# Layer 1's attention: weighted values summed eight heads at a time, more weight buffers, and the end of a half as a stage of its own

## The chip, the cores and the metric

The kernel runs on one core of one Trainium2 chip. Its time is the device time of one launch in microseconds (us). Of several runs the median is given; one more execution was taken with the hardware profiler, and all rows of the profile come from that one.

## What is computed

Two layers run over 16 sequences (b) of 512 tokens and 128 channels, all in float32. Each layer is a layer norm, then the sum of a sequence mixer, a feed-forward part and the input itself.

```python
# layer 0: a memory MLP trained by a scan over chunks (the mixer), and:
q, k, v = split(conv(x) @ wqkv.T + bqkv)                   # 16 heads of 8 channels
ctx  = softmax(q @ k.T / sqrt(8)) @ v                      # no mask
x    = layernorm(x + ctx @ wo.T + bo)
x    = layernorm(x + sum_e probs[e] * (relu(x @ w1[e]) @ w2[e]))   # 8 experts, all of them

# layer 1
ctx  = causal_attention(q, k, v);  q2 = conv(ctx)
out  = causal_attention(q2, k, v) @ out_w.T + out_b        # a second look at the same k and v
ffn  = top-8 of 32 experts, gathered and scattered by token
```

So layer 0 has one attention per sequence and layer 1 has two, both masked so that a token sees itself and what is before it.

## The kernel before

The program is written as Python generators, called stages here. Class `Turns` runs them: in one turn every stage that is alive is advanced by one step. Each stage has a priority. Those of priority 0 step first, then those of priority 1, then the others from 2 to 6. TensorE gets its instructions in exactly this order (`ORDERED`); for the other engines a scheduler orders them, with the edges that `issue_after` adds: what stages of priority 1 and up give VectorE comes behind the last maximum of priority 0 (`newest`), and what stages of priority 2 and up give GpSimd comes behind the last mask of priority 1 (`cleared`). The program before has 1281 turns, counted as it is built.

Attention is done in halves of 8 heads (c is 0 or 1), and each half is looked at twice:

- The first look is `tops` with `largest`, priority 0. A step computes scores with the queries as weights (L190, `s<-kx,qx`) and takes the maximum of each row on VectorE (L387 with the mask in one instruction, or L395 and L396). Its maxima are carried into two extra rows of the queries.
- The second look is `back` with `weighted`, priority 1. A step computes the scores again, transposed (`s<-qx,kx`), and ScalarE takes the exponential into a weight tile `e` (L461). In layer 1 GpSimd then zeroes what the mask hides (L465).

Each look has one score tile of two banks in PSUM, so a step of a look cannot begin before the engine that reads the scores has finished with the step before it. `widths` says what a step covers. In layer 0 a half takes 16 steps of two heads and 512 queries. In layer 1 the mask shortens it: four steps of two heads by 512 queries, four of two heads by 384, two of four heads by 256, and one of eight heads by 128, 11 steps in all. The looks of layer 1 follow each other without a gap: a sequence takes 4 halves, or 44 turns (`TBB`).

The weighted values are TensorE matmuls of 32 columns each (`pc<-e,vp`), four heads side by side in the four column groups of the array. A float32 matmul appears in the profile as two passes, so four heads are eight rows. They are summed in one bank, `pc`, of which there is one (lock `ctx`). Function `tail(n)` issues them: behind the scores of a step, if four heads or more are waiting in the list `old`, their four values go out; I call this a visit. Weight tiles come from a ring of three. At the end of a half the same stage, still at priority 1, issues what is left (four heads a turn), copies `pc` to `cs` (L437, ScalarE), transposes it (`tpc`, L241) and divides by the sums on VectorE (L485, L486). Meanwhile the next half's `weighted` has begun, and steps later in the same turn.

The large filler of TensorE's time is layer 0's experts, stage `ffn` of priority 6, which runs through nearly all of the program. A unit of it is `phe<-x1T,ew` (L190, 512 columns, with a relu on ScalarE, L565) or the four matmuls of `pye<-ew,hTe` (L573). How many units a turn gets is a matter of credit in estimated nanoseconds:

```python
credit[0] = min(credit[0] + TURN - load_ns[0], 4000)       # TURN = 2750
n = int(max(credit[0] + 500, 0) // 1000)
```

So a turn in which other stages gave TensorE much work gets fewer units, and the turns behind it get more. Where `ffn` is not at work, `fill` adds matmuls that nobody reads.

Stage `middle` (layer 0's end and layer 1's routing) uses pool `mid`, which is open from the end of the scan (turn 481) to turn 1167. Then `moe` takes its place; it gathers and scatters tokens with DMAs that GpSimd issues.

Of the kernel before, what the change touches and what calls it, by code (L numbers as in the profile page):

```python
# [9 lines left out]
F32 = mybir.dt.float32  # L10
# [7 lines left out]
P = 128  # L18
# [55 lines left out]
def bc(ap, axis, n):  # L74

    u = ap.unsqueeze(axis)
    shape = list(u.shape)
    shape[axis] = n
    return u.to_broadcast(shape)
# [3 lines left out]
def network(ctx: ExitStack, tc: tile.TileContext, a, out):  # L83
# [26 lines left out]
    def load(pool, name, shape):  # L110
        t = pool.tile(shape, F32, bufs=1, name="sb_" + name)
        nc.sync.dma_start(t, a[name])
        return t
# [21 lines left out]

    pools, done, locks, clock, newest, cleared, held, read, cell = {}, {}, set(), [0], [None], [None], [0], [0], []

    def mark(*m):
        done[m] = clock[0]

    def after(*marks, lag=0):

        while not all(m in done and clock[0] >= done[m] + lag for m in marks):
            yield

    def acquire(name):
        while name in locks:
            yield
        locks.add(name)
# [7 lines left out]
    def room():  # L157

        while held[0] >= pools["work"]:
            yield  # L160
# [6 lines left out]
    def drop():  # L167

        read[0] += 1
# [12 lines left out]
    def mm(o, lhsT, rhs, start=True, stop=True):  # L182
        n = int(np.prod(rhs.shape[1:]))
        if lhsT.dtype == FR:
            load_ns[0] += 0.5 * (0.45 * n + 105)
        else:
            t = 0.42 * n if lhsT.shape[-1] == 32 and n >= P else 2 * max(0.834 * n, 110)
            load_ns[0] += t
            array_ns[0] += t
        nc.tensor.matmul(o, lhsT=lhsT, rhs=rhs, start=start, stop=stop)  # L190
# [46 lines left out]
    def turn4(src, name="tp"):  # L237

        tp = work(name)
        for t in range(4):  # L240
            nc.tensor.transpose(tp[:, t * P : (t + 1) * P], src(t), ident)  # L241
        load_ns[0] += 900
        array_ns[0] += 900
        return tp
# [12 lines left out]

    def ends(stage, name):
        yield from stage
        mark(name)  # L260

    def idle(n):
        for _ in range(n):
# [87 lines left out]
    def widths(causal):  # L351

        for i in range(TB):
            n = S if not causal else S - i * P
            per = {S: 1, 3 * P: 1, 2 * P: 2, P: 4}[n]
            for t in range(0, NH, per):
                yield i, n, per, t
# [58 lines left out]
            )  # L416
        yield

    def weighted(slot, vp, c, causal, cn):

        q, k, _ = slot
        yield from acquire("p2")
        cnv = cn.rearrange("p t (a c j d) -> p (t a) c j d", c=2, j=2, d=DH)
        old, ends = [], []
        got = []

        def values(heads):
            for kt, n, t, r, e in heads:
                g = 2 * (t % 2) + r
                j = t // 2  # L430
                mm(
                    got[0][32 * g : 32 * g + 32, S - n :], vp[:, kt, 4 * g + 2 * c + j, :], e,
                    start=(kt == 0 and j == 0), stop=(kt == TB - 1 and j == 1),
                )
            if kt == TB - 1 and t == NH - 1:
                cs = att.tile([P, S], F32, tag="cs", bufs=1, name="cs")
                nc.scalar.copy(cs, got[0])  # L437
                locks.remove("ctx")
                ends.append(cs)

        def tail(n):
            if not got and "ctx" not in locks:
                locks.add("ctx")
                got.append(pools["ps"].tile([P, 512], F32, tag="ctx", bufs=1, name="pc"))
            for _ in range(n):
                if got and len(old) >= 4:
                    locks.add("values")
                    values([old.pop(0) for _ in range(4)])

        for kt, n, per, t in widths(causal):  # L450
            while len(old) >= 4 and not got and "ctx" in locks:
                yield
            s = pools["ps"].tile([P, 2, 512], F32, tag="p2", bufs=pools["p2"], name="s2")
            sv = s[:, :, 0 : per * n].rearrange("p r (i n) -> p r i n", i=per)
            for u in range(per):
                for r in range(2):
                    rr = slice(64 * r, 64 * r + 64)
                    mm(sv[:, r, u, :], k[rr, t + u, kt * P : (kt + 1) * P], q[rr, t + u, S - n :])
            tail(2)
            e = att.tile([P, 2, 512], F32, tag="e", bufs=pools["e"], name="e")  # L460
            nc.scalar.activation(e[:, :, 0 : per * n], s[:, :, 0 : per * n], AF.Exp, scale=SCALE)  # L461
            ev = e[:, :, 0 : per * n].rearrange("p r (i n) -> p r i n", i=per)
            if causal:
                for r in range(2):
                    cleared[0] = nc.gpsimd.affine_select(  # L465
                        out=ev[:, r, :, 0:P], in_=ev[:, r, :, 0:P], pattern=[[0, per], [1, P]],
                        compare_op=ALU.is_ge, fill=0.0, base=0, channel_multiplier=-1,
                    )
            for u in range(per):
                for r in range(2):  # L470
                    old.append((kt, n, t + u, r, ev[:, r, u, :]))
            yield
        locks.remove("p2")
        free_slots.append(slot)
        while old:
            tail(1)
            yield
        cs = ends[0]
        yield from room()
        held[0] += 1  # L480
        tp = turn4(lambda t: cs[:, t * P : (t + 1) * P], "tpc")
        yield
        tv = tp.rearrange("p (b j x) -> p b j x", j=2, x=16)
        rec = sm.tile([P, TB * NG, 2], F32, tag="rec", name="rec")
        nc.vector.reciprocal(rec, tv[:, :, :, DH])  # L485
        nc.vector.tensor_tensor(cnv[:, :, c], tv[:, :, :, 0:DH], bc(rec, 3, DH), ALU.mult)  # L486
        drop()
        yield
# [10 lines left out]
    def ffn(b):  # L499
# [106 lines left out]
        yield  # L606
        nc.sync.dma_start(x1d[0, b], flat(ac))
        mark("ffn", b)
        yield

# [5 lines left out]
    att = main.enter_context(tc.tile_pool(name="att", bufs=1))  # L616
    fa = main.enter_context(tc.tile_pool(name="fa", bufs=2))
    ff = main.enter_context(tc.tile_pool(name="ff", bufs=1))
    ps = main.enter_context(tc.tile_pool(name="psum", bufs=1, space=PSUM))
    pools.update(ps=ps, p1=1, p2=1, work=3, e=3, pairs=True)  # L620
    Wt = Pack(load(fa, "pb", [P, sum(PB.values())]), PB)
    cell.append(Wt.t)
    row.update(load_rows(fa, "rows0", ROWS0))
# [416 lines left out]
    def tops(layer, b, i, c):  # L1040
        yield from after(("rows", layer, b, i))
        got, z = [], live[layer, b]
        yield from take(free_slots, got)
        z[i, c] = got[0]
        rows_in(got[0], c, z["r2"] if i else z["rq"], z["rk"])
        yield from idle(3)
        yield from largest(got[0], layer == 1)
        mark("tops", layer, b, i, c)

    def back(layer, b, i, c):  # L1050
        yield from after(("tops", layer, b, i, c), lag=4)
        yield from after(("vals", layer, b))
        z = live[layer, b]
        if c == 0:
            z["cn"] = (l1 if layer else fa).tile([P, TB, D], F32, tag="cn", bufs=2, name="cn")
        yield from weighted(z[i, c], z["vp"], c, layer == 1, z["cn"])
        mark("back", layer, b, i, c)

    def post0(b):
        yield from after(("back", 0, b, 0, 0), ("back", 0, b, 0, 1))  # L1060
# [28 lines left out]
    def experts0():  # L1089
        for b in range(B):  # L1090
            yield from ffn(b)

    TA = 32
    turns = Turns(
        [(60, 6, experts0())]
        + [(b * TA, 4, front0(b)) for b in range(B)]
        + [(b * TA + 4 + 16 * c, 0, tops(0, b, 0, c)) for b in range(B) for c in range(2)]
        + [(b * TA + 30 + 16 * c, 1, back(0, b, 0, c)) for b in range(B) for c in range(2)]
        + [(b * TA + 60, 4, post0(b)) for b in range(B)]
    )  # L1100
    with tc.tile_pool(name="p0", bufs=1) as p0:
        stage = norm0(p0)
        turns.stages.append((0, 3, ends(stage, "norm0")))
        turns.run(until=lambda: ("norm0",) in done)
    with tc.tile_pool(name="scan", bufs=1) as s1:
        turns.stages.append((turns.turn, 3, ends(scan(s1), "scan")))
        turns.run(until=lambda: ("scan",) in done)


# [286 lines left out]
    )  # L1396
    with tc.tile_pool(name="mid", bufs=1) as mid:
        turns.stages += [(t0 + b * TBB, 4, middle(mid, b)) for b in range(B)]
        turns.run(until=lambda: ("xw", B - 1) in done)
    with tc.tile_pool(name="mo", bufs=2) as mo:  # L1400
        turns.stages.append((turns.turn, 3, moe(mo)))
        turns.stages += [(turns.turn, 5, total(b)) for b in range(B)]
        turns.run()
# [111 lines left out]
```

## Time and profile before

| | us |
|---|---|
| median of 3 runs | 4081.94 |
| lowest and highest | 4064.09, 4087.86 |
| the profiled execution, its own time | 4071.58 |
| its span | 4069.8 |

| engine | busy us | share of the span |
|---|---|---|
| TensorE (PE) | 3646.2 | 90% |
| VectorE (DVE) | 2368.5 | 58% |
| ScalarE (ACT) | 2201.1 | 54% |
| GpSimd (POOL) | 1681.3 | 41% |

A row of the profile names the line, the engine, the operation and out<-in. A line such as L190 is that of a helper (`mm`), so the matmuls are told apart by their tiles: `s<-kx,qx` first look, `s<-qx,kx` second look, `pc<-e,vp` weighted values. Matmuls overlap in the array and their ends are modelled, so what one costs is read from the distance between starts.

### The profile page before, as it was taken

To read this page: it belongs to the slowest core of one execution; us is meant where nothing else is said; L and a number is where in the kernel's file an instruction comes from. 1 tells how busy PE (TensorE), PEld (TensorE's weight loads), DVE (VectorE), ACT (ScalarE), POOL (GpSimd) and SP (SyncE) were. 2 spreads that over 40 slices of the span, in tenths; PEclk is the share of its full clock that TensorE was granted. 3 is DMA by queue.
4 is the path that set the end of the run, shared out by engine and by line. 5 is a ranking of instruction groups with operands and counts; after the bars stand their busy time and mean duration, and the time that the engine had idled before them with its cause. 6 is when DMAs were issued, how large, how long until landed. Compare 5 with 4: busy or idle time off the path is not lost.

```text
span 4069.8 us, 62831 instructions
## 1 busy us (share of the span) xinstructions
PE 3646.2 (90%) x22668; PEld 1974.2 (49%) x22668; DVE 2368.5 (58%) x5165; ACT 2201.1 (54%) x3686; POOL 1681.3 (41%) x2598
## 2 busy tenths in 40 slices
PE   5998899888999998999999999999999999987877
PEld 2544454444544444455555555555555555543443
DVE  3575656665565555564566655666656666676651
ACT  1355655566557775555555555555555555542332
POOL 7334534455333544134333442333334423434563
PEclk6799999999999999999999999999999999997888
DMA  4222222122223333333333333333333343323334
GB/s 155 62 62 62 70 57 77 57 68 64 75 75 93 108 96 108 101 105 110 90 111 103 114 81 111 108 100 95 111 101 107 87 117 106 94 69 98 70 69 131
DMA packets 271222, 374.22 MB, mean 92 GB/s; under 512 B 42392, under 2 KB 116800, under 8 KB 270144
## 3 DMA queue, kind: packets, MB, share of 16 engines
q1 hardware_dynamic: 263744, 363.38, 30.7%
q0 software_dynamic: 7168, 6.82, 1.0%
q8 instruction: 180, 2.95, 0.3%
q14 instruction: 130, 1.06, 0.1%
HBM read 236.85 MB, written 133.25 MB: 91 GB/s over the span
## 4 chain that ended last, share of the span: by engine, by line
PE 62%; DVE 15%; POOL 7%; ACT 6%; DMA 5%; issue 5%; SPq 0%; POOLq 0%; ACTq 0%; DVEq 0%
PE s L190 16%; PE pye L573 10%; PE phe L190 9%; PE pc L190 9%; DVE nm L396 7%; DVE s L395 3%; ACT e L461 2%; PE pgr L190 2%; POOL e L465 1%; PE tp L241 1%; DVE s L387 1%; PE fill L197 1%; PE po L190 1%; PE pj L190 1%; DMA fin<-ao 1%
## 5 line engine op out<-in xcount | busy, mean ns | idle before, releaser
L461 ACT ACTIVATE e<-s 128x1024 f32<-128x1024 f32 (+1 forms) x1216 | 1190.6, 979 | 836.5 <-PE s L190 796.0
L396 DVE TENSOR_REDUCE nm<-s 128x2 f32<-128x1024 f32 (+1 forms) x704 | 861.9, 1224 | 664.6 <-PE s L190 657.5
L387 DVE CUSTOM_DVE_ANT_0 s<-s,sb_const 128x512 f32<-128x512 f32 (+1 forms) x1024 | 647.6, 632 | 663.9 <-PE s L190 646.4
L465 POOL TENSOR_SCALAR_AFFINE_SELECT e<-e 128x128 f32<-128x128 f32 (+2 forms) x1408 | 464.4, 363 | 1140.9 <-ACT e L461 1133.0
L190 PE MATMUL s<-kx,qx 64*128 64x512 f32 (+3 forms) x3072 | 627.6, 435 | 180.9 <-DVE nm L396 99.4
L190 PE MATMUL pc<-e,vp 128*32 128x512 f32 (+3 forms) x6144 | 712.4, 511 | 52.4 <-POOL e L465 51.3
L190 PEld LDWEIGHTS s<-kx,qx 64*128 64x128 f32 x3072 | 278.7, 189 | 754.0 <-issue 288.9
L573 PEld LDWEIGHTS pye<-ew,hTe 128*128 128x128 f32 x4096 | 517.2, 193 | 212.1 <-issue 195.6
L573 PE MATMUL pye<-ew,hTe 128*128 128x128 f32 x4096 | 572.7, 283 | 0.5 <-DVE cn L486 0.5
L190 PE MATMUL phe<-x1T,ew 128*128 128x512 f32 x1024 | 553.5, 624 | 6.9 <-DVE vp L345 1.9
L190 PE MATMUL s<-qx,kx 64*128 64x512 f32 (+3 forms) x3072 | 536.1, 373 | 21.1 <-ACT e L461 15.3
L565 ACT ACTIVATE hTe<-phe,sb_cols 128x512 f32<-128x512 f32 x512 | 353.1, 690 | 272.5 <-PE phe L190 272.1
L190 PEld LDWEIGHTS s<-qx,kx 64*128 64x128 f32 x3072 | 290.7, 190 | 124.2 <-issue 64.6
L581 POOL TENSOR_TENSOR ac<-ac,y 128x512 f32<-128x512 f32 x128 | 165.4, 1292 | 387.0 <-ACT y L580 386.8
L395 DVE TENSOR_TENSOR s<-s,sb_const 128x256 f32<-128x256 f32 (+1 forms) x384 | 199.4, 519 | 178.8 <-PE s L190 166.5
L190 PEld LDWEIGHTS pc<-e,vp 128*32 128x32 f32 x6144 | 137.6, 109 | 264.7 <-issue 152.2
L190 PEld LDWEIGHTS phe<-x1T,ew 128*128 128x128 f32 x1024 | 158.2, 193 | 113.3 <-issue 84.6
L580 ACT ACTIVATE y<-pye,pr 128x128 f32<-128x128 f32 x512 | 146.8, 368 | 51.0 <-PE pye L573 50.0
L387 DVE DVE_READ_ACCUMULATOR2_ANT nm<- 128x1 f32 x1024 | 145.0, 142 | 0.0
L197 PE MATMUL fill<-sb_pb,sb_const 128*128 128x512 f32 (+3 forms) x256 | 135.9, 621 | 8.8 <-DMA sb_pb<-in_pb 7.8
L437 ACT COPY cs<-pc 128x512 f32<-128x512 f32 x96 | 56.2, 585 | 61.1 <-PE pc L190 59.4
L410 ACT CAST m<-tpm 16x512 fp32r<-16x512 f32 x96 | 54.6, 569 | 59.4 <-PE tpm L408 59.4
(285 smaller groups left out, 4049.0 us busy)
## 6 DMA issues: line engine op xcount, KB each, us to landing
ew<-in_ew SPq DMA_DIRECT2D x256, 256.0 KB
kx<-rk SPq DMA_DIRECT2D x192, 256.0 KB
qx<-rq SPq DMA_DIRECT2D x128, 256.0 KB
rq<-hi SPq DMA_DIRECT2D x64, 256.0 KB
rq<-lo SPq DMA_DIRECT2D x64, 256.0 KB
rk<-hi SPq DMA_DIRECT2D x64, 256.0 KB
rk<-lo SPq DMA_DIRECT2D x64, 256.0 KB
qx<-r SPq DMA_DIRECT2D x64, 256.0 KB
```

The costliest lines, as they stand in the source:

```text
L190: nc.tensor.matmul(o, lhsT=lhsT, rhs=rhs, start=start, stop=stop)
L197: nc.tensor.matmul(o[:, 0:n], lhsT=ident, rhs=cell[0][:, 0:n], start=True, stop=True)
L387: newest[0] = nc.vector.tensor_tensor_reduce(out=sv[:, r, 0, :], in0=sv[:, r, 0, :], in1=row["caus"][:, S - n :], scale=1.0, scalar=-BIG, ...
L395: nc.vector.tensor_tensor(dg, dg, bc(row["caus"][:, S - P :], 1, per), ALU.add)
L396: newest[0] = nc.vector.tensor_reduce(nm[:, qt, :, t : t + per], sv, AX.X, ALU.max)
L437: nc.scalar.copy(cs, got[0])
L461: nc.scalar.activation(e[:, :, 0 : per * n], s[:, :, 0 : per * n], AF.Exp, scale=SCALE)
L465: cleared[0] = nc.gpsimd.affine_select(out=ev[:, r, :, 0:P], in_=ev[:, r, :, 0:P], pattern=[[0, per], [1, P]], compare_op=ALU.is_ge, fill= ...
L565: nc.scalar.activation(hs[i], ph, AF.Relu, bias=col("fb", i))
L573: nc.tensor.matmul(pye[0][:, t, :], lhsT=h[:, t * P : (t + 1) * P], rhs=w2[e][:, f, :], start=(f == 0 and t == 0), stop=(f == 3), skip_gro ...
L580: nc.scalar.mul(y[:, t, :], pye[0][:, t, :], pr[:, t, e : e + 1])
L581: nc.gpsimd.tensor_tensor(ac, ac, y, ALU.add)
```

## The change

Three things are changed. While pool `mid` is open, values go out eight heads at a time (two groups of four behind each other) and not four (`heads`). In the same stretch the weight tiles come alternately from the ring of three in `att` and from a second ring of three in `mid`; the set `lent` holds the heads whose weights lie in `mid`, and the pool is not closed before they are used. And in both layers, for the whole program, the end of a half becomes a stage `summed` of priority 2, which starts in the turn after `weighted` is done: in a turn it steps behind both looks. Its values go out up to eight heads a turn as well.

```diff
-        def tail(n):
+        def tail(least):
             if not got and "ctx" not in locks:
                 locks.add("ctx")
                 got.append(pools["ps"].tile([P, 512], F32, tag="ctx", bufs=1, name="pc"))
-            for _ in range(n):
-                if got and len(old) >= 4:
-                    locks.add("values")
+            if got and len(old) >= least:
+                locks.add("values")
+                for _ in range(min(len(old) // 4, 2)):
                     values([old.pop(0) for _ in range(4)])
 
-        for kt, n, per, t in widths(causal):
-            while len(old) >= 4 and not got and "ctx" in locks:
+        for i, (kt, n, per, t) in enumerate(widths(causal)):
+            while len(old) >= pools["heads"] and not got and "ctx" in locks:
                 yield
...
-            tail(2)
-            e = att.tile([P, 2, 512], F32, tag="e", bufs=pools["e"], name="e")
+            tail(pools["heads"])
+
+            pool = pools["weights"][i % len(pools["weights"])]
+            e = pool.tile([P, 2, 512], F32, tag="e", bufs=3, name="e")
...
         locks.remove("p2")
         free_slots.append(slot)
+        turns.stages.append((turns.turn, 2, ends(summed(old, tail, last, c, cnv), name)))
+
+    def summed(old, tail, last, c, cnv):
+
         while old:
-            tail(1)
-            yield
-        cs = ends[0]
+            tail(4)
+            yield
+        cs, = last
         yield from room()
...
-    pools.update(ps=ps, p1=1, p2=1, work=3, e=3, pairs=True)
+    pools.update(ps=ps, p1=1, p2=1, work=3, weights=[att], heads=4, pairs=True)
...
     with tc.tile_pool(name="mid", bufs=1) as mid:
         turns.stages += [(t0 + b * TBB, 4, middle(mid, b)) for b in range(B)]
+        pools.update(weights=[att, mid], heads=8)
         turns.run(until=lambda: ("xw", B - 1) in done)
+        pools.update(weights=[att], heads=4)
+        turns.run(until=lambda: not lent)
```

More of the change, by code (lines that the diff above doesn't have):

```diff
@@ L136, in network @@
     pools, done, locks, clock, newest, cleared, held, read, cell = {}, {}, set(), [0], [None], [None], [0], [0], []
+    lent = set()
     def mark(*m):
@@ L259, in ends @@
         yield from stage
-        mark(name)
+        mark(*name)
     def idle(n):
@@ L417, in largest, with weighted @@
         yield
-    def weighted(slot, vp, c, causal, cn):
+    def weighted(slot, vp, c, causal, cn, name):
         q, k, _ = slot
@@ L423, in weighted @@
         cnv = cn.rearrange("p t (a c j d) -> p (t a) c j d", c=2, j=2, d=DH)
-        old, ends = [], []
+        old, last = [], []
         got = []
         def values(heads):
-            for kt, n, t, r, e in heads:
+            for head in heads:
+                kt, n, t, r, e = head
+                lent.discard(id(head))
                 g = 2 * (t % 2) + r
@@ L438, in values @@
                 locks.remove("ctx")
-                ends.append(cs)
-        def tail(n):
+                last.append(cs)
+        def tail(least):
             if not got and "ctx" not in locks:
@@ L471, in weighted @@
                     old.append((kt, n, t + u, r, ev[:, r, u, :]))
+                    if pool is not att:
+                        lent.add(id(old[-1]))
             yield
@@ L1055, in back @@
             z["cn"] = (l1 if layer else fa).tile([P, TB, D], F32, tag="cn", bufs=2, name="cn")
-        yield from weighted(z[i, c], z["vp"], c, layer == 1, z["cn"])
-        mark("back", layer, b, i, c)
+        yield from weighted(z[i, c], z["vp"], c, layer == 1, z["cn"], ("back", layer, b, i, c))
     def post0(b):
@@ L1102, in network @@
         stage = norm0(p0)
-        turns.stages.append((0, 3, ends(stage, "norm0")))
+        turns.stages.append((0, 3, ends(stage, ("norm0",))))
         turns.run(until=lambda: ("norm0",) in done)
     with tc.tile_pool(name="scan", bufs=1) as s1:
-        turns.stages.append((turns.turn, 3, ends(scan(s1), "scan")))
+        turns.stages.append((turns.turn, 3, ends(scan(s1), ("scan",))))
         turns.run(until=lambda: ("scan",) in done)
```

## The prediction

> **What bounds the kernel now.** I read the page first (span, engine table, the rows of the 40 slices), then the windows of three stages, then the waits of the stage that is changed, then its timeline.
>
> ```profile
> PE 3646.2 (90%) x22668; PEld 1974.2 (49%) x22668; DVE 2368.5 (58%) x5165; ACT 2201.1 (54%) x3686; POOL 1681.3 (41%) x2598
> PEclk6799999999999999999999999999999999997888
> 1600.00:3690.00 2090.00, 1938.41 (x13233) 1077.44 (x13230) 1265.39 (x3388) 1157.25 (x1751) 743.25 (x1586) 0.99 0.35 102
> 3690.00:4069.80 379.80, 294.48 (x1562) 138.97 (x1560) 182.43 (x501) 121.71 (x167) 199.89 (x302) 0.81 0.35 86
> ```
>
> TensorE carries the program. From 1600 to 3690 us, where layer 1 runs beside the experts, it is busy 1938 of 2090 us (the columns are length, PE, PEld, DVE, ACT, POOL, granted clock). No other engine is above 61% there. But PE is not the only limit: it works in order, and each turn opens with the first look, which waits for VectorE's maxima of the turn before.
>
> Two looks at the timeline of PE in that stage (start us, us, instruction; in brackets PE's idle time and who ended it), the end of one half and then two turns of 256-wide scores:
>
> ```profile
> 2387.84 0.44 PE L190 MATMUL s<-kx,qx 64*128 64x384 f32 x2
> 2388.12 0.56 PE L190 MATMUL s<-qx,kx 64*128 64x128 f32 x8
> 2388.61 0.64 PE L190 MATMUL pc<-e,vp 128*32 128x256 f32 x8
> 2389.18 1.13 PE L190 MATMUL phe<-x1T,ew 128*128 128x512 f32 x2
> 2390.23 0.44 PE L190 MATMUL s<-kx,qx 64*128 64x384 f32 x2
> 2391.08 0.41 PE L190 MATMUL pc<-e,vp 128*32 128x128 f32 x2 [0.41 <-POOL e L465]
> 2391.67 0.42 PE L190 MATMUL pc<-e,vp 128*32 128x128 f32 x6 [0.18 <-POOL e L465]
> 2392.02 0.50 PE L190 MATMUL s<-qx,kx 64*128 64x512 f32 x2
> ...
> 2394.40 0.44 PE L190 MATMUL s<-kx,qx 64*128 64x384 f32 x2
> 2394.77 0.43 PE L190 MATMUL pc<-e,vp 128*32 128x128 f32 x8
> 2395.13 0.51 PE L190 MATMUL s<-qx,kx 64*128 64x512 f32 x2
> ```
>
> ```profile
> 2363.35 0.90 DVE L395 TENSOR_TENSOR s<-s,sb_const 128x256 f32<-128x256 f32 x2 [1.89 <-PE s L190]
> 2364.28 1.22 DVE L396 TENSOR_REDUCE nm<-s 128x4 f32<-128x1024 f32 x1
> 2365.65 0.50 PE L190 MATMUL s<-kx,qx 64*128 64x256 f32 x4 [0.33 <-DVE nm L396]
> ```
>
> In the first, the half's last weights (eight heads, 128 wide) have just been made. Its values stand ahead of the next half's look, and wait for GpSimd's two masks: 1.79 us pass from one look to the other (2390.23 to 2392.02), where the next turn takes 0.73 (2394.40 to 2395.13). In the second, PE has too little to do: the turn from 2362.80 to 2365.65 is 2.85 us long because VectorE takes 0.90 and 1.22 us.
>
> **The change part by part.**
>
> *The wait at a half's end.* In the new order these values stand behind the next half's second look, a turn later, when the masks (0.64 us each at 512 elements) are long done. I took the distance from first to second look in all 102 turns of this kind between turns 481 and 1167: the least is 0.72 us, most are 0.73, some 1.3 to 1.8, and all they have above the least is 22.7 us. The waits view says the same from above: PE and PEld wait 9.2 and 26.4 us for the masks there (first two lines; some lies under running matmuls).
>
> ```profile
> PEld pc L190 <- POOL e L465: 26.4, 67, 1.2
> PE pc L190 <- POOL e L465: 9.2, 37, 1.0
> ...
> PEld pc L190 <- POOL e L465: 59.4, 52, 5.3
> PE pc L190 <- POOL e L465: 42.1, 27, 4.9
> ```
>
> That is -23 us (range -30 to -10).
>
> *Fewer visits.* Layer 1 has 512 visits before; the built program has 283, since 229 are joined. What does a visit cost? Distances between starts, undisturbed: from a 512-wide second look to its values 0.32, from the first value to what follows 1.00, and its two passes stand 0.45 apart. From a second look straight to an expert matmul it is 0.33 to 0.42. Two groups in one visit do not exist before; their nearest row is the distance of passes, so the second group costs 0.90, at most a whole visit's 1.00, at least its streaming (0.88). A joined visit then saves 0.09 us at 512 columns. In the same way 0.10 at 384 (0.78 a visit) and 0.12 at 256 (0.57). At 128 it saves 0.31: two visits between the looks (0.73 against 0.28 without, each) become one of about 0.59. Sum 0.62 a half, 64 halves: 40 us of PE's time.
>
> A rule of the Trainium skill would give more. "TensorEngine Tiling (Array Packing)", Key Properties, says that a change of tiling mode drains the array, and "TensorE: Matmul & The Clock Gate", Single matmul latency, puts the drain at about 175 ns. By that estimate 229 visits of two changes each give 80 us. The rows say less: between the 64-row look and the 128-row expert stands a change anyway (the 0.33 to 0.42), so a visit adds one, of about 0.1. I take the rows.
>
> Nor do the 40 us all lie on the path. I cut the built order of both programs at the ends of turns and added up PE's distances for each turn. A turn can't be shorter than VectorE allows; the shortest seen, by what the first look does, are 2.15 us (512), 1.82 (384), 2.85 (256) and 3.49 (128). Taking for each turn the larger of PE's sum plus 0.11 and this floor, turns 560 to 1130 come to 1703 us before (measured: 1770) and 1685.5 after, and turns 490 to 1240 fall by 21. So half of the 40 is lost in turns that VectorE sets: -20 us (range -40 to +5).
>
> *A turn's load is lumpier.* A visit at 512 columns now takes 1.9 us in one turn and none in the next three. The experts' credit evens it: the built order has one unit or none in such a turn and two or three in the others, and the floors are in the sum above. A second rule speaks against it: "TensorE: Matmul & The Clock Gate", What's actually happening, halves the clock after an idle window of about 3.4 us. The thinnest turns built have 0.70 us of PE's work against a floor of 2.15, so 1.4 us idle. The window's row shows 0.99 granted with such turns in it. By the row nothing; by the rule nothing either, unless two such follow each other: one turn a half at half clock would be +45 (64 x 0.7). I take 0.
>
> *Weight buffers.* The second ring lets four steps wait. The exponential never waits for a buffer in the waits of before (it waits for PE's scores), so it saves nothing; it is there to make eight heads possible, and new waits on it have two turns of slack. 0.
>
> *What is moved at a half's end.* The copy `cs` (0.59 us) now stands behind the exponential of the same turn on ScalarE. The transposes, a reciprocal (0.35) and a product (0.42) come a turn later. Queued behind the copy are relus, which have a turn. The next values need the bank that it empties: in layer 1 three turns later, in layer 0 one turn later, where look, look and exponential cover it (about 2.4 us after the turn's second look began against a shortest turn of 1.8 and 0.7 more). If that cover fails, up to 0.5 us in 32 halves: +16. Layer 0 has no mask, and its distances of the same kind spread by 0.8 us in all; PE's sum falls 6 us, the sum with floors rises 6. I take 0 (-6 to +16). The marks `back` come a turn later, so conv and rows of the second attention do too; the looks follow each other without gaps either way, and the program has 1282 turns for 1281: +1 to +3, take +2. DMA issues are as many on SP (1848) and POOL (96), and each is moved by a turn at most. Fills: 126 for 128.
>
> *After turn 1167* values go out by four again, and only the reordering acts. There GpSimd also issues gathers and scatters of about 1 us each, and PE waits 59.4 and 42.1 us for masks (the last two lines above). 16 us of that are at halves' ends. But GpSimd is what is short there, and from 3970 us on the chain of waits goes through the last additions (`fin`). The masks that are no longer waited for at the end will be waited for two steps on. Half: -8 (-16 to +5).
>
> Sum: -23 - 20 + 0 + 2 - 8 = -49. Against the profiled execution, 4071.6 - 49 = 4022.6. It lies 10 us under the median; against that, 4081.9 - 49 = 4033. I say 4030.
>
> **The rivals.**
>
> 1. *Only the order counts.* Visits are free because VectorE's floor fills whatever PE gives up. For: PE waits for the maxima in every 256- and 128-wide turn. Against: most 512- and 384-wide turns exceed their floor. Then -23 - 8 + 2 = -29: 4053.
>
> 2. *All of it lands.* 40 + 23 + 16 = 79, and less idle time behind it: 4000. For: turns measure 67 us above my sum, so there are waits that I do not name. Against: the 128-wide turn is at 3.49 in nearly every half.
>
> 3. *Slower: the lump delays the second look.* In the turns that get two or three expert units ScalarE has up to two relus of 0.69 and four products of 0.37 beside an exponential of 1.02, and runs them in order. If the exponential comes late, the next second look waits, and everything on PE behind it. Price: one relu's worth, 0.69 us, at each of the 4 visits of 64 halves is 177 us; a third of them makes +59, and the sum +10 to +40: 4110. It decides from 0.2 us a visit (49/256). For: ScalarE waits for PE in most turns, so it is phase that counts, not load. Against: it is 55% busy, and turns with two units exist before without excess.
>
> 4. *The change does less than it says.* The built order shows 229 joined visits, so no.
>
> **How the numbers follow.** The main case has 0.45, rival 1 0.22, rival 2 0.15, rival 3 0.12, and 0.06 for a sum of nothing (a shift given back in the tail). What a measurement of this kernel can tell from no change is about 0.5%, 20 us. The main case and rival 2 are faster by more, and most of rival 1: 0.76. Within 0.5%: a quarter of rival 1, the last case and a bit of rival 3: 0.14. Slower: 0.10. The range runs from rival 2 (with its floor gone too, 3985) to a small loss, 4088.
>
> **What would show it.** Right: no idle time of `pc` behind L465 between the looks at a half's end, and from look to look 0.28 there; the wait of `pc` for POOL under 15 us in the middle stage; 16 passes of `pc` in a row at 1.9 us; a sequence of 44 turns in about 134 us where it took 136.6 (`ao`, 2042.6 to 3408.5 over ten). Wrong: a sequence in 136 us or more; PE's waits for DVE `nm` grown by what the waits for POOL fell; a wait of the second look for ACT `e` that was not there before (rival 3).

## The result, and the profile after

| | before | after |
|---|---|---|
| median, us | 4079.29 (4 runs) | 4031.53 (4 runs) |
| lowest and highest | 4064.09 to 4087.86 | 4027.2 to 4034.16 |
| ratio, 95% interval | | 0.9878 (0.9858 to 0.9899) |
| span of the profiled execution | 4069.8 | 4025.5 |

The change makes the kernel 1.2% faster. The forecast was 4030. That it came out nearly to the microsecond is luck: the middle gained more than was forecast, layer 0 and the tail less, and the errors cancel, as the stages show.

I cut both spans at three marks: the end of the scan (the load of layer 1's weights is issued), the first and the last store to `xw`. The rows below are windows of the kernel before, then of the kernel after; the columns are stretch, length, PE, PEld, DVE, ACT, POOL busy us, granted clock, DMA share, GB/s.

```profile
0.00:1576.40 1576.40, 1391.79 (x7762) 747.76 (x7763) 907.26 (x1257) 909.77 (x1750) 725.56 (x697) 0.94 0.27 78
1576.40:1661.80 85.40, 79.31 (x448) 39.74 (x446) 47.72 (x89) 48.61 (x71) 28.15 (x31) 0.98 0.47 147
1661.80:3682.20 2020.40, 1879.57 (x12899) 1047.24 (x12898) 1226.53 (x3302) 1120.84 (x1698) 727.12 (x1566) 0.99 0.35 101
3682.20:4069.80 387.60, 295.57 (x1562) 139.47 (x1562) 186.96 (x518) 121.88 (x168) 200.43 (x304) 0.80 0.35 88
```

```profile
0.00:1601.00 1601.00, 1386.83 (x7746) 747.60 (x7747) 905.35 (x1258) 908.58 (x1748) 722.10 (x698) 0.93 0.27 77
1601.00:1679.40 78.40, 75.59 (x449) 39.04 (x448) 45.81 (x87) 47.37 (x72) 27.37 (x31) 1.00 0.53 160
1679.40:3635.90 1956.50, 1808.74 (x12878) 1054.29 (x12878) 1225.36 (x3299) 1112.18 (x1699) 723.90 (x1562) 0.97 0.37 104
3635.90:4025.50 389.60, 285.31 (x1594) 137.47 (x1594) 189.25 (x524) 123.62 (x170) 202.02 (x308) 0.84 0.35 88
```

I call the four stages layer 0, passage, middle and tail. Layer 0 lost 24.6 us, the passage gained 7.0, the middle gained 63.9, the tail lost 2.0: together -44.3, the difference of the spans. In the middle PE is busy 71 us less for as many matmuls (12878 records for 12899), and DVE, ACT and POOL are busy as long as before, within 9 us. In layer 0 PE's idle time (length less busy) grew from 184.6 to 214.2 us.

The end of a half in the timeline of PE, after the change:

```profile
2389.01 0.56 PE L192 MATMUL s<-qx,kx 64*128 64x128 f32 x8
2389.50 1.07 PE L192 MATMUL pc<-e,vp 128*32 128x256 f32 x16
2390.50 1.16 PE L586 MATMUL pye<-ew,hTe 128*128 128x128 f32 x8
2391.59 0.45 PE L192 MATMUL s<-kx,qx 64*128 64x384 f32 x2
2391.87 0.40 PE L192 MATMUL s<-qx,kx 64*128 64x512 f32 x2
2392.20 1.12 PE L192 MATMUL phe<-x1T,ew 128*128 128x512 f32 x2
...
2394.43 0.39 PE L192 MATMUL s<-qx,kx 64*128 64x512 f32 x2
2394.75 0.64 PE L192 MATMUL pc<-e,vp 128*32 128x128 f32 x16
2395.32 1.13 PE L192 MATMUL phe<-x1T,ew 128*128 128x512 f32 x2
...
2402.24 0.66 PE L192 MATMUL s<-kx,qx 64*128 64x128 f32 x8 [1.03 <-DVE nm L398]
2402.72 0.42 PE L192 MATMUL s<-qx,kx 64*128 64x384 f32 x2
2403.07 1.92 PE L192 MATMUL pc<-e,vp 128*32 128x512 f32 x16
2404.92 0.70 PE L192 MATMUL phe<-x1T,ew 128*128 128x512 f32 x1
```

At the end of a half nothing stands between the looks any more: 0.28 us from one to the other (2391.59 to 2391.87). The last eight values go out at 2394.75, a turn later, and wait for nobody. The row at 2402.24 shows what is left: the first look waits for VectorE. The waits of PE in the middle, with the passage before it, first before and then after:

```profile
PE s L190 <- DVE nm L396: 47.8, 101, 2.7
PE s L190 <- issue: 24.4, 23, 1.6
PE s L190 <- DVE nm L387: 24.3, 44, 1.5
```

```profile
PE s L192 <- DVE nm L398: 68.6, 91, 2.2
PE s L192 <- DVE nm L389: 41.7, 42, 1.5
...
PE s L192 <- issue: 2.3, 3, 0.8
...
PEld pc L192 <- POOL e L472: 3.5, 12, 0.4
```

The wait of `pc` and its weight loads for the masks (35.6 us before) fell to 3.5, and PE's wait for VectorE grew from 72.1 to 110.3 us. That overstates what VectorE takes back: the looks' waits for which the profile names nobody (`issue`) fell by 22 us at the same time, and PE's idle time in passage and middle is 146.9 us before and 150.6 after. What got shorter is the time in which PE counts as busy.

By the width of the first look, the turns of the middle add up to 753, 689, 341 and 235 us before (512, 384, 256 and 128) and to 740, 625, 341 and 246 after. So the gain lies in the 384-wide turns, in which the halves end. The 256-wide turns, whose median is 2.85 us both times, gave nothing: VectorE sets them, as the forecast said.

### The profile page after: what moved, and what is told of

It is laid out like the page before. It is cut to its first block, busy times and chain, and to the rows that moved or that the text cites. A ratio compares the mean times of both kernels' runs of the same rounds, so it can differ in the third digit from the quotient of the medians.

```text
span 4025.5 us, 62790 instructions
## 1 busy us (share of the span) xinstructions
PE 3556.5 (88%) x22664; PEld 1978.4 (49%) x22664; DVE 2365.8 (59%) x5165; ACT 2191.8 (54%) x3686; POOL 1675.4 (42%) x2598
## 5 line engine op out<-in xcount | busy, mean ns | idle before, releaser
L192 PE MATMUL pc<-e,vp 128*32 128x512 f32 (+3 forms) x6144 | 665.4, 520 | 39.3 <-POOL e L472 35.5
L192 PE MATMUL s<-qx,kx 64*128 64x512 f32 (+3 forms) x3072 | 512.0, 359 | 46.8 <-ACT e L468 29.8
L192 PEld LDWEIGHTS pc<-e,vp 128*32 128x32 f32 x6144 | 155.5, 112 | 278.8 <-issue 191.3
L199 PE MATMUL fill<-sb_pb,sb_const 128*128 128x512 f32 (+2 forms) x252 | 134.5, 623 | 8.8 <-DMA sb_pb<-in_pb 7.8
L205 POOL TENSOR_SCALAR rs_t<-ss 128x4 f32<-128x4 f32 (+1 forms) x56 | 11.4, 203 | 168.6 <-ACT sq L257 167.2
```

The costliest lines, as they stand in the source:

```text
L199: nc.tensor.matmul(o[:, 0:n], lhsT=ident, rhs=cell[0][:, 0:n], start=True, stop=True)
L205: nc.gpsimd.tensor_scalar(t, src, scale, eps, ALU.mult, ALU.add)
```

## Experiments

The theory: the middle gains because (a) at a half's end PE no longer waits for the masks, and (b) visits are joined; layer 0 loses because the end of a half comes a turn later there and other steps meet. The rivals: eight heads alone carry the gain; the order does, joined or not; layer 0's loss is chance, or comes from the values' place behind the second look.

Stages of all kernels, from one profiled execution each, in us. The ratio is to the kernel before, run beside it on the same chip. The mark between passage and middle shifts: in the four kernels whose layer 1 is that of before (before, order0_only, before_scan_later, before_post_later) the middle takes 2011.3 to 2024.1 us, and passage and middle together 2105.8 to 2108.0. So where a few us of the middle matter, I give the sum too.

| kernel | layer 0 | passage | middle | tail | median | ratio, 95% interval |
|---|---|---|---|---|---|---|
| before | 1576.4 | 85.4 | 2020.4 | 387.6 | 4079.29 | |
| after | 1601.0 | 78.4 | 1956.5 | 389.6 | 4031.53 | 0.9878 (0.9858 to 0.9899) |
| order_only | 1608.3 | 86.5 | 1973.3 | 388.0 | 4053.73 | 0.9932 (0.9911 to 0.9954) |
| eight_only | 1578.3 | 89.6 | 1996.6 | 382.3 | 4046.43 | 0.9919 (0.9889 to 0.9949) |
| layer1_only | 1575.1 | 88.2 | 1959.0 | 371.1 | 3996.11 | 0.9798 (0.9768 to 0.9828) |
| order0_only | 1601.9 | 83.9 | 2024.1 | 372.2 | 4086.51 | 1.0023 (1.0005 to 1.0041) |
| before_no_last_mask | 1578.2 | 86.8 | 1995.8 | 362.7 | 4039.2 | 0.9919 (0.9893 to 0.9944) |
| order1_single | 1576.0 | 85.3 | 1905.2 | 511.9 | 4081.2 | 1.0014 (1.0005 to 1.0023) |
| order1_joined | 1580.0 | 82.8 | 1972.6 | 373.1 | 4010.69 | 0.9826 (0.9800 to 0.9852) |
| before_joined_end | 1574.3 | 86.5 | 2039.3 | 367.9 | 4059.82 | 0.9948 (0.9922 to 0.9974) |
| before_scan_later | 1584.0 | 84.8 | 2022.4 | 384.5 | 4088.26 | 1.0025 (1.0014 to 1.0036) |
| after_scan_later | 1626.3 | 86.0 | 1948.3 | 363.6 | 4028.08 | 0.9883 (0.9855 to 0.9910) |
| before_post_later | 1582.4 | 95.9 | 2011.3 | 389.6 | 4075.8 | 0.9991 (0.9981 to 1.0000) |
| layer0_late | 1598.6 | 77.9 | 1954.3 | 387.8 | 4023.12 | 0.9873 (0.9841 to 0.9906) |

### The parts of the change by themselves

The order at the end, without the eight heads:

```diff
-        pools.update(weights=[att, mid], heads=8)
```

> The end of a half is a stage of its own behind both looks in both layers, but values go out four heads at a time throughout. Theory 1 (the order at the end carries the gain of layer 1: 23 us of waiting for masks, and some 20 us because the last two visits are joined between look and expert; eight heads add about 20): layer 1's stage -45 us, layer 0 +25 as in the changed kernel, so about 4059. Rival (eight heads carry it): layer 1's stage -15, layer 0 +25, so about 4090.

Measured: middle 1973.3, that is -47 (with the passage -46), layer 0 +32, in all 4053.7. Theory 1's number for the middle (-45) held.

Eight heads, without the order:

```diff
-        turns.stages.append((turns.turn, 2, ends(summed(old, tail, last, c, cnv), name)))
+        yield from ends(summed(old, tail, last, c, cnv), name)
```

> Eight heads at a time and the second ring as in the change, but the end of a half stays inline ahead of the next half's second look (its left values may go out eight heads in one turn). Theory 1: layer 1's stage -20 to -30 us, the wait for masks between the looks stays, layer 0 as before, so about 4055. Rival (eight heads carry it): layer 1's stage -60, so about 4020.

Measured: middle -24 (with the passage -20), layer 0 as before, 4046.4. The rival wanted -60. The wait for the masks is still there (20.7 and 10.2 us in PEld's and PE's waits in passage and middle), as it must be with the inline end. Here the last two visits are joined between the looks, which by itself costs time (before_joined_end, below), so the parts do not simply add: -47 and -24 for the two alone, -64 together.

The whole change, in layer 1 alone:

```diff
-        turns.stages.append((turns.turn, 2, ends(summed(old, tail, last, c, cnv), name)))
+        if causal:
+            turns.stages.append((turns.turn, 2, ends(summed(old, tail, last, c, cnv), name)))
+        else:
+            yield from ends(summed(old, tail, last, c, cnv), name)
```

> The whole change in layer 1, but in layer 0 the end of a half stays inline. Theory 1 (layer 0's +25 us come from the new order there, which moves the scan and its readout against the halves): layer 0 as before, layer 1's stage -70, so about 4010. Rival (the +25 are the chance of one execution, or come from a shared cause): about 4031, as the changed kernel.

Measured: 3996.1, layer 0 at 1575.1, middle at 1959.0. Leaving layer 0 alone is worth 35 us against the change as it was made: 26 in layer 0 and 18.5 in the tail, less 10 in the passage and 2.5 in the middle (in the profiles; the tail's share is not explained, see below). It is the fastest of all kernels here, 2.0% under the kernel before.

The order in layer 0 alone:

```diff
-        turns.stages.append((turns.turn, 2, ends(summed(old, tail, last, c, cnv), name)))
+        if not causal:
+            turns.stages.append((turns.turn, 2, ends(summed(old, tail, last, c, cnv), name)))
+        else:
+            yield from ends(summed(old, tail, last, c, cnv), name)
...
-        pools.update(weights=[att, mid], heads=8)
```

> The end as a stage of its own in layer 0 alone, layer 1 as before. Theory 1: layer 0 +25 us, nothing else, so about 4104. Rival (layer 0's loss is chance): 4079.

Measured: layer 0 1601.9, +25.5 as expected; so the loss is not chance. In all it is only 7 to 9 us slower than before, since its tail was 15 us shorter. That is not explained (see below).

### What the order at the end gains

First the wait alone. In the kernel before, the masks of a half's last step are left out:

```diff
-            if causal:
+            if causal and kt < TB - 1:
                 for r in range(2):
                     cleared[0] = nc.gpsimd.affine_select(
```

> The kernel before, with the two masks of a half's last step left out (so the values of those keys are summed unmasked); nothing is moved. Theory 1 (the order at a half's end gains 23 us because PE no longer waits for these masks): layer 1's stage -23 us (2020 to about 1997 between the first and the last xw), the wait of pc for POOL there nearly gone, and some 10 to 16 us in the tail, so about 4045. Rival (the end's order gains by fewer changes of mode alone): layer 1's stage as before, about 4075.

Measured: middle -24.6, and the wait of `pc` for GpSimd in passage and middle falls from 35.6 to 4.0 us, with nothing moved:

```profile
PE pc L190 <- POOL e L465: 0.7, 3, 0.3
PEld pc L190 <- POOL e L465: 3.3, 10, 0.5
```

The time from first to second look at the halves' ends, above the least of 0.72 us, falls in all from 23.4 to 1.0 us in passage and middle. The 23 us of the forecast are thus confirmed by taking the cause away. The tail fell by 25 us too, but GpSimd is short there and has less to do in this kernel.

Then the order without the joined last visit, in layer 1 alone (besides the line below, the edits of layer1_only and order_only):

```diff
-                for _ in range(min(len(old) // 4, 2)):
+                for _ in range(1):
```

> The end as a stage of its own in layer 1 alone, values four heads at a time throughout, and at the end too one group of four a turn, so the last two visits are not joined. Theory 1 (of the 47 us that the order gave layer 1's stage, 23 are the wait and the rest is the joined last visit): -23 to -28 us in that stage, about 4050. Rival (the place behind the second look is what counts, joined or not): -45, about 4030.

A miss: 4081. The bank `pc` is now released one turn later, and the next half, which has four heads waiting by then, gives up a turn for it (`while len(old) >= ... and "ctx" in locks`); this is read from the code. The built program has 1341 turns where the kernel before has 1281. The middle looks short (1905) only because the looks fall behind `middle` and are caught up in the tail (512). What the order gains is lost in 60 more turns. The run does not tell wait and joining apart, but it shows why the stage at the end has to send all eight at once.

With the last visit joined again, and otherwise the same (against order1_single):

```diff
-                for _ in range(1):
+                for _ in range(min(len(old) // 4, 2)):
```

> As the run before with one group a turn, but both groups of the end go out in one turn, so that the bank for the sums is free a turn earlier and no look waits for it (1281 turns where that one had 1341). The end as a stage of its own in layer 1 alone, values four heads at a time elsewhere. Theory 1 (wait 24 us and joined last visit 20 to 26): layer 1's stage -45 to -50 us, layer 0 as before, about 4030. Rival (what the order gave in layer 1 needs the order in layer 0 too): about 4055.

Measured: 4010.7, middle 1972.6 (-47.8), layer 0 1580. So the order in layer 1 alone gives the middle all that it gave in order_only. Of the 47.8, 24.6 are the wait; the other 23 are what remains for the last visits, joined and out of the way between the looks. Against this kernel, layer1_only has eight heads besides: 14 us in the middle (8 with the passage), 14.6 us in the medians.

Joining without moving, in the kernel before:

```diff
         while old:
-            tail(1)
+            tail(2)
             yield
```

> The kernel before, inline end and all, except that the eight heads left at a half's end go out in one turn, between the looks. Theory 1 (a visit of 128 columns costs 0.45 us there, and two joined about 0.69): 0.21 us in each of 64 halves, -14 us in layer 1's stage, the wait for the masks as before; about 4065. Rival (joining saves nothing, the order does): layer 1's stage as before, 4078.

A miss in the stage that it was meant for: the middle is 19 us longer, not 14 shorter. Both groups now wait for the masks of the step just done:

```profile
PE pc L190 <- POOL e L465: 16.0, 53, 1.3
...
PEld pc L190 <- POOL e L465: 51.3, 136, 1.6
```

67.3 us against 35.6. Before, the second group went out a turn later and was free of it. So joining pays only behind the second look, where the masks are done. In the medians this kernel is 20 us faster all the same (4059.82 against 4080.43). The profiled execution doesn't show why: there its tail is 20 us shorter, which only makes up for the middle.

### What layer 0 loses

Three kernels with the order in layer 0 end their scan at 1601.0, 1608.3 and 1601.9 us; seven without it, and without a shift of other steps, at 1574 to 1580. Is it the place of the values, or which steps fall into one turn?

The scan begun one turn later, in the kernel before and in the changed one:

```diff
-        turns.stages.append((turns.turn, 3, ends(scan(s1), ...
+        turns.stages.append((turns.turn + 1, 3, ends(scan(s1), ...
```

> The kernel before, with the scan begun one turn later, so that its steps meet other steps of layer 0's halves. Theory 1 (layer 0's loss of 25 us is a matter of which steps of scan and readout fall into one turn): layer 0 changes by 5 to 30 us in either direction by this alone. Rival (the new order costs layer 0 for itself): layer 0 within 5 us of 1576 to the scan's end, 4077.

> The changed kernel, with the scan begun one turn later. Theory 1 (which steps meet): the wait of 13 us for POOL's rq at 1334 us goes or moves, and layer 0 ends 10 to 30 us away from 1601. Rival (the new order costs layer 0 for itself): about 1601 to 1605, 4031 to 4035 in all.

Measured: 1584.0 (+8) and 1626.3 (+25). In the second kernel the shift also alters part of what is computed, for a reason that I did not follow up; only the length of its layer 0 is used. So a shift of one turn moves layer 0 by 8 us in the first kernel, and by 25 in the second, whose wait for `rq` did not go either (21.5 us in four waits, the longest 11.0). In neither phase was the new order as good as the old.

The stage behind a half begun one turn later, in the kernel before:

```diff
-        yield from after(("back", 0, b, 0, 0), ("back", 0, b, 0, 1))
+        yield from after(("back", 0, b, 0, 0), ("back", 0, b, 0, 1), lag=1)
```

> The kernel before, with layer 0's stage behind a half (post0) begun one turn later, as the change does by marking a half's end a turn later; nothing else is moved. Theory 1 (layer 0's loss comes from what then falls into one turn with the readout): to the scan's end 15 to 30 us more than 1576, about 4095. Rival (the values behind the second look cost layer 0 for themselves): within 8 us of 1576, about 4078.

Measured: 1582.4, +6. Theory 1 in this form falls: the later mark alone is not the cause, though it may account for a part.

The last run keeps the end of layer 0's halves inline and ahead of the look, and only begins it one turn later (against layer1_only):

```diff
         else:
+            yield
             yield from ends(summed(old, tail, last, c, cnv), name)
```

> The whole change in layer 1. In layer 0 the end of a half is inline and ahead of the next look, as before, but begins one turn later, in the turn in which the change's own stage begins. Theory 1 (layer 0 loses because the whole end comes a turn later, so other steps meet in a turn): to the scan's end about 1600 us as in the changed kernel, in all about 4020. Rival (it loses because the values stand behind the second look): to the scan's end 1575 to 1584, in all about 3996.

Measured: layer 0 1598.6, and 4023.1 in all, against 1575.1 and 3996.1 without the `yield`. Here the values stand between the looks as they always stood. So it is not their place behind the second look that costs layer 0, but that the end (values, copy, transposes, division) comes one turn later. PE's waits from 200 us to the scan's end, in the kernel before, in the changed kernel and in this one:

```profile
PE tp L241 <- POOL rq L966: 6.0, 2, 5.5
```

```profile
PE tp L243 <- POOL rq L979: 17.1, 2, 13.0
```

```profile
PE tp L243 <- POOL rq L983: 17.1, 2, 13.0
```

The transposes of the readout (`rq`) wait once for 13.0 us in the changed kernel, and again for 13.0 us in layer0_late: the same stall, built into the order. It is in order_only and order0_only too (17.1 us in two waits, as here), and not in layer1_only (6.1). The timeline shows what is at work in it: ScalarE's squares of two readouts and GpSimd's chain behind them (three sums and products of 1.26 us for `yq`, then those of `rq`), while PE stands in front of its transposes. This is 11 of the 25 us. The other 14 are spread over waits that differ between the two kernels: the looks' wait for `e` is 13.0 us in the kernel before, 23.1 in the changed one and 15.7 in layer0_late. I can't name one cause for them. The granted clock is not what the two share: it stands at half for 191 us of layer 0 before, for 225 in the changed kernel, but only for 198 in layer0_late, which is as slow.

## Why the prediction was right, and where it was not

- *The wait at a half's end*: forecast -23, shown as -24.6 by leaving the masks out. The distance that it was read from (0.73 us from look to look, with excess over it) was the right one.
- *Fewer visits*: forecast 40 us of PE's time, half of it lost to VectorE, -20. The runs give about -39: -23 for the last visits (order1_joined less the wait) and about -16 for eight heads (1956.5 against order_only's 1973.3 gives 16.8; layer1_only against order1_joined 13.6; with the passage 24.9 and 8.2). The step that failed is the price of a visit. In the changed trace a joined visit takes, from its first value to the next matmul, 1.85 us at 512 columns, 1.43 at 384, 1.00 at 256 and 0.57 at 128 (medians). I had put the second group at 0.90 us for 512 columns; it is 0.86. More weight lay elsewhere: a second look that follows values was followed by an expert only after 0.43 us (2392.02 to 2392.45 in the trace before), one that follows a first look after 0.33 (2391.87 to 2392.20 after). In the trace before, the matmul that ends these 0.43 us is

```profile
2392.45 1.16 PE L573 MATMUL pye<-ew,hTe 128*128 128x128 f32 x8
```

  I had seen "0.33 to 0.42" and priced all at the low end, so two visits between the looks cost 0.2 us a half more than I counted. With these rows a half saves 3 x 0.14 + 2 x 0.45 + 2 x 0.10 - 0.57 = 0.95 us, 61 us in 64 halves instead of 40. The estimate from drains, 0.35 us for each joined visit, is not borne out: two visits of the same columns save 0.14 by joining. That a part is lost again was right, in about the size given: 61 less 39 is 22, against 20. That it is VectorE that takes these 22 is argued from its fixed turns and not measured.
- *The signs*: those named for being right all came, a sequence in 132 us among them (`ao`, 2052.0 to 3372.5 over ten). But one named for being wrong came too: PE's waits for `nm` grew by 38 us where those for POOL fell by 32. It was a bad sign: PE's idle time as a whole grew by only 4 us there, and the gain lies in its busy time.
- *A lumpier turn*: forecast 0, by a rule that was read too kindly. The granted clock of the middle is 0.97 for 0.99; it stood at half for 109 us in 19 stretches, and for 44 us in 8 before. Around one of them (two windows, and a row of PE's timeline):

```profile
1829.99:1833.40 3.41, 0.81 (x8) 0.42 (x6) 3.25 (x8) 2.33 (x6) 2.16 (x5) 1.00 0.08 32
1833.40:1847.10 13.70, 12.62 (x66) 6.31 (x67) 8.49 (x21) 3.07 (x3) 6.73 (x13) 0.50 0.52 166
1835.33 2.79 PE L192 MATMUL pc<-e,vp 128*32 128x384 f32 x16
```

  The visit of 384 columns takes 2.72 us to the next start (1838.05) where 1.43 is the median. The Trainium skill ("TensorE: Matmul & The Clock Gate", What's actually happening) names an idle window of about 3.4 us for this; here PE had been busy 0.81 us of the 3.41 before it, so the window need not be all idle. In the traces before and after, from 150 us on, I cut the time into stretches of 3.41 us, the steps of the granted clock there, and took those at full clock. Where PE was busy less than 40% of such a stretch, the clock was half in the next one in 48 cases of 48; from 40 to 60% in 45 of 92; above 60% in 4 of 1972. So thin turns can have a price. What the eight heads add to it is not isolated: order0_only, with layer 1 as before, has 102 us at half clock in its middle, and that stage is only 3.7 us longer than before. Rival 3 did not occur: the second look's waits for `e` did not grow (PEld 3.1 us before, 1.5 after, in passage and middle).
- *What is moved at a half's end in layer 0*: forecast 0, at most +16. It cost 25 us, outside of the bounds that I set. I priced the queues that the moved copy stands in, and found them covered (in the changed trace the loads of `pc` wait 5.0 us for `cs` in all of layer 0); I didn't price that the steps of scan, readout and experts meet in other turns when an end moves by one. For steps that share turns by a hand-made calendar, 25 us on 1600 is the size of that effect here, and the PE sums with floors (+6) did not foretell it.
- *The tail*: forecast -8; in the profiles it is +2.0. It takes 371 to 390 us among after, order_only, layer1_only, order1_joined and layer0_late, which have the same code there, and 372 to 390 among the four kernels with layer 1 as before. I found no rule for it. What the reordering does in the tail stays open.

So the forecast of 4030 was right as a sum, and that was luck: passage and middle gave -71 where -43 was forecast, against +25 not foreseen in layer 0 and a tail 10 us longer than forecast. The waits and visits that it named are the ones that gained. "All of it lands" has the number of the middle (-63 for -64), but not the reason: more was saved than it counted, and a part was lost again.

## What to carry to other kernels

Where one stage's end stands ahead of the next stage's start on an in-order engine, move it behind: what it waits for gets a turn to finish, and the next chain begins at once; but see first who holds the buffer that it frees (one turn more, and 60 turns are lost). Price a matmul by what it follows and not by its own row: here the same look held up the next matmul for 0.43 or for 0.33 us. And apply a change stage by stage: the same reordering gained 48 us in layer 1's stage and lost 25 in layer 0, and only the run that left layer 0 out shows the 2.0%. (What layer 0's order costs the whole program depends on the tail: 35 us between after and layer1_only, 7 to 9 between order0_only and before.)

## What the hardware showed that I had not expected

A matmul group's cost depends on the group before it: after four-column-group values, a 64-row look of 512 columns holds up the next 128-row matmul for 0.43 us from its start, after another 64-row look 0.33. The values' shape is not needed for it: behind the 128-row transposes `tpc` the look took 0.43 too (54 cases in the trace before). And the sixteen passes of a joined visit cost 0.57, 1.00, 1.43 and 1.85 us at 128 to 512 columns: 0.43 us for each 128 columns and 0.14 us that doesn't depend on them (a single visit's 0.57, 0.78 and 1.00 at 256, 384 and 512 fit 0.21 for each 128 columns and the same 0.14), so that this 0.14 us is all that joining two visits of the same columns saves by itself.
